# First chunk of a fused two-layer kernel: the order of its loads, its mean and variance by matmul alone, and later weight centring

## The chip, the cores and the metric

The kernel runs on one core of one Trainium2 chip. The metric is device time in microseconds (us) for one execution. The engines are named as the profile names them: PE is TensorE (matmuls), PEld its weight load, DVE is VectorE, ACT is ScalarE, POOL is GpSimd, and SP is the engine that issues most of the DMAs.

## The reference

The input x has 2 sequences of 1024 tokens with 256 channels. Eight blocks follow one another, four in each of two layers; pairs of them stand in a residual sum. In short:

```python
x = x + time_mix(adapter(x, profile_ids))         # layer 0: adapter chosen per sequence, linear recurrence
x = x + moe(mlp_with_chosen_part(x, ids))         # layer 0: 8 experts, 2 per token
x = x + local_attention(dense_or_sparse_attention(x))   # layer 1
x = x + squared_relu_ffn(adapter2(x, ids))        # layer 1
```

The change touches the first block. Its adapter is chosen by a profile number, one for each sequence (`itok_B_0_6`, two numbers below 8):

```python
z = relu(hidden @ Wd[id] + bd[id])                # 256 -> 128
y = hidden + z @ Wu[id] + bu[id]                  # 128 -> 256
mu = mean(y); var = mean((y - mu) ** 2)           # over the 256 channels
out = (y - mu) * rsqrt(var + 1e-5) * g[id] + b[id]
```

Its output goes into a token-shift mixer, four small projections, and the recurrence.

## The kernel before

x is kept transposed and resident: 128 partitions, two halves of the 256 channels, 2048 tokens (`x`, `[P, 2, T]`). The first block works on four chunks of 512 tokens (`CK`), two for each sequence. `tmix_in` runs three steps in a staggered way: while `adapt` works on chunk i, `mix` works on chunk i-1 and `project` on chunk i-2. Each step is a generator, and a string of letters says which one goes on next (`together`). A scheduler then sets the final order of each engine's queue from the written order and the dependences; each engine takes its own queue strictly from the front.

`setup` makes the constants and loads `vecs`, the packed vectors, on SP's queue. `program` then loads the four chunks of x on ACT's queue (L1796). `load_adapter0` reads the two profile numbers into a register of SP (`value_load`, L116; two dependent loads each) and with each number loads the packed weights of that sequence, `d0_0` and `d0_1` (L118). `load_attn0` loads `wa`, the weights of mixer and projections (L124), and `lvl`, a small table of masks (L126), which POOL then spreads 16 times (L129). `load_late` follows with `wf` and two more number reads (L156). Twelve zero fills of DRAM tables close this part of SP's queue (L1812).

`centre_weights` takes the mean out of the up-projection of each sequence, so that the adapter's output needs no second mean: DVE reduces `wu` and subtracts (L168 to L170), PE averages the bias `bu` with the matrix `avg`, which holds 1/256 everywhere (L173), and DVE subtracts that too (L174, L175). It does so for both sequences before the first chunk. `centre_values` does the same for the value weights in `wa` (L360 to L362), when `i == 1`.

`adapter_steps` is the adapter of one chunk. POOL adds the two channel halves of x (`both`, L202). PE makes `pz` (L205) and ACT the relu `z` (L207). PE makes the mean of x by one matmul of `avg` with `both` (L209), and DVE subtracts it from x (L212). PE makes the up-projection `py` (L217), DVE adds it and the bias (L219). ACT squares both halves in one instruction (L221), POOL adds the two squared halves (L223), PE makes the variance, four matmuls of 128 tokens each into columns of `nv` (L227). ACT takes the root and DVE the reciprocal (`inverse_root`, L181 and L183). PE transposes it to a row for each token (L234), DVE multiplies (L237) and ACT adds the offset into `q` (L238). The tiles named `ad` are two PSUM banks used in turn; `both` is one buffer. The profile counts two PE passes for each fp32 matmul.

Of the kernel before, what the change touches and what calls it, by code (L numbers as in the profile page):

```python
# [9 lines left out]
F32 = mybir.dt.float32  # L10
# [8 lines left out]
P = 128  # L19
B = 2  # L20
# [42 lines left out]
def tiles(tc, **how):  # L63

    return tc.tile_pool(reuse_waits="tile", **how)
# [24 lines left out]
def setup(k, ctx):  # L90
    nc, tc, ins = k.nc, k.tc, k.ins
    cp = ctx.enter_context(tiles(tc, name="const", bufs=1))
    k.vecs = cp.tile([P, NVEC], F32, name="vecs")
    nc.sync.dma_start(out=k.vecs, in_=ins["vecs"])
    k.ident = cp.tile([P, P], F32, name="ident")
    make_identity(nc, k.ident)
    k.avg = cp.tile([P, P], F32, name="avg")
    nc.vector.memset(k.avg, 1.0 / C)

    k.sel64 = cp.tile([P, 2], F32, name="sel64")  # L100
    nc.vector.memset(k.sel64, 0.0)
    for h in range(2):
        nc.vector.memset(k.sel64[64 * h : 64 * h + 64, h : h + 1], 1.0 / 64)
    k.ones = cp.tile([P, P], F32, name="ones")
    nc.vector.memset(k.ones, 1.0)
    k.eps = {}
    for n, e in (("ln", 1e-5), ("gn", 0.00064)):
        k.eps[n] = cp.tile([P, 1], F32, name=f"eps_{n}")
        nc.vector.memset(k.eps[n], e)


def load_adapter0(k, pool):
    nc, ins = k.nc, k.ins
    k.d0 = []
    for b in range(B):
        i = nc.sync.value_load(ins["ids"][0:1, b : b + 1], min_val=0, max_val=7)  # L116
        t = pool.tile([P, ND0], F32, name=f"d0_{b}")
        nc.sync.dma_start(out=t, in_=ins["d0"][bass.ds(i, 1)].rearrange("o p f -> p (o f)"))  # L118
        k.d0.append(t)


def load_attn0(k, pool, raw):
    k.wa = pool.tile([P, NWA], F32, name="wa")
    k.nc.sync.dma_start(out=k.wa, in_=k.ins["wa"])  # L124
    lvl = raw.tile([P, 6, P // 4], U8, name="lvl")
    k.nc.sync.dma_start(out=lvl, in_=k.ins["lvl"])  # L126

    k.lvl = pool.tile([P, 6, 2 * S // P, P // 4], U8, name="lvls")
    k.nc.gpsimd.tensor_copy(k.lvl, lvl.unsqueeze(2).to_broadcast([P, 6, 2 * S // P, P // 4]))  # L129


def load_cond2_0(k, pool):
# [26 lines left out]
        k.d2.append(t)  # L159


def centre_weights(k, sp, pp, packed, table, n_wu, n_bu):

    nc = k.nc
    for t in packed:
        wu, bu = (part(t, table, n) for n in (n_wu, n_bu))
        m = sp.tile([P, 2], F32, name="cwm")
        nc.vector.reduce_sum(m[:, 0:1], wu, axis=AX.X)  # L168
        nc.vector.tensor_scalar_mul(m[:, 0:1], m[:, 0:1], 1.0 / C)
        nc.vector.tensor_scalar(wu, wu, m[:, 0:1], None, ALU.subtract)  # L170
        pb = pp.tile([P, CK], F32, name="nv")
        for c in range(2):
            nc.tensor.matmul(pb[:, 0:1], lhsT=k.avg, rhs=bu[:, c : c + 1], start=c == 0, stop=c == 1)  # L173
        nc.vector.tensor_copy(m[:, 1:2], pb[:, 0:1])  # L174
        nc.vector.tensor_scalar(bu, bu, m[:, 1:2], None, ALU.subtract)  # L175
# [8 lines left out]
    return rs  # L184


def adapter_steps(k, sp, pp, x, ch, dst, tables, names, hid):

    nc = k.nc
    packed, table = tables
    n_wd, n_wu, n_bd, n_bu = names
    b, t0 = ch // 2, ch * CK
    ts = slice(t0, t0 + CK)
    nb = CK // P
    wd = part(packed[b], table, n_wd, 2)
    wu, bd, bu, g, bb = (part(packed[b], table, n) for n in (n_wu, n_bd, n_bu, "g", "b"))  # L200
    both = sp.tile([P, CK], F32, name="both")
    nc.gpsimd.tensor_add(both, x[:, 0, ts], x[:, 1, ts])  # L202
    pz = pp.tile([P, CK], F32, name="ad", bufs=2)
    for c in range(2):
        nc.tensor.matmul(pz, lhsT=wd[:, c, :], rhs=x[:, c, ts], start=c == 0, stop=c == 1)  # L205
    z = sp.tile([P, CK], F32, name="z")
    nc.scalar.activation(z, pz, AF.Relu, bias=bd)  # L207
    pm = pp.tile([P, CK], F32, name="ad", bufs=2)
    nc.tensor.matmul(pm, lhsT=k.avg, rhs=both, start=True, stop=True)  # L209
    y = sp.tile([P, 2, CK], F32, name="y")  # L210
    for c in range(2):
        nc.vector.tensor_sub(y[:, c, :], x[:, c, ts], pm)  # L212
    yield
    py = [pp.tile([P, CK], F32, name="ad", bufs=2) for c in range(2)]
    for c in range(2):
        hs = slice(0, hid) if hid == P else slice(c * hid, (c + 1) * hid)
        nc.tensor.matmul(py[c], lhsT=wu[hs, c * P : (c + 1) * P], rhs=z[hs], start=True, stop=True)  # L217
    for c in range(2):
        nc.vector.scalar_tensor_tensor(y[:, c, :], py[c], bu[:, c : c + 1], y[:, c, :], ALU.add, ALU.add)  # L219
    sq = sp.tile([P, 2, CK], F32, name="nsq")  # L220
    nc.scalar.activation(sq, y, AF.Square)  # L221
    both = sp.tile([P, CK], F32, name="both")
    nc.gpsimd.tensor_add(both, sq[:, 0, :], sq[:, 1, :])  # L223
    yield
    pv = pp.tile([P, nb], F32, name="nv")
    for j in range(nb):
        nc.tensor.matmul(  # L227
            pv[:, j : j + 1], lhsT=both[:, j * P : (j + 1) * P], rhs=k.avg[:, 0:1], start=True, stop=True
        )
    rs = inverse_root(k, sp, pv, "ln")  # L230
    yield
    pb = pp.tile([P, CK], F32, name="ad", bufs=2)
    for j in range(nb):
        nc.tensor.transpose(pb[:, j * P : (j + 1) * P], rs[:, j : j + 1].to_broadcast([P, P]), k.ident)  # L234
    for c in range(2):
        t = sp.tile([P, CK], F32, name="t")
        nc.vector.scalar_tensor_tensor(t, y[:, c, :], g[:, c : c + 1], pb, ALU.mult, ALU.mult)  # L237
        nc.scalar.activation(dst[:, c, :], t, AF.Identity, bias=bb[:, c : c + 1])  # L238
    yield


def adapted(k, sp, pp, x, it, tables, names, hid):

    q = it["q"] = sp.tile([P, 2, CK + 1], F32, name="q", bufs=2)
    if it["ch"] % 2:
        k.nc.vector.tensor_copy(q[:, :, 0:1], it["prev"]["q"][:, :, CK : CK + 1])
    else:
        k.nc.vector.memset(q[:, :, 0:1], 0.0)
    yield from adapter_steps(k, sp, pp, x, it["ch"], q[:, :, 1:], tables, names, hid)


def together(order, **steps):
# [6 lines left out]
def tmix_in(k, x, r, kk, w, v):  # L259
# [10 lines left out]
    with (  # L270
# [2 lines left out]
        tiles(tc, name="mxp", bufs=1, space=PSUM) as pp,  # L273
    ):

        centre_weights(k, sp, ap, k.d0, D0, "wu", "bu")

        def bank(i, shape=(P, CK)):
            return pp.tile(list(shape), F32, name=f"f{i}")

        def adapt(it):
            return adapted(k, sp, ap, x, it, (k.d0, D0), ("wd", "wu", "bd", "bu"), P)

        def mix(it):
            cur = it["q"][:, :, 1:]
# [69 lines left out]
        def centre_values():  # L355


            wv = part(wa, WA, "v").rearrange("p (g d) -> p g d", d=64)
            mean = sp.tile([P, 8], F32, name="wvm")
            nc.vector.reduce_sum(mean, wv, axis=AX.X)  # L360
            nc.vector.tensor_scalar_mul(mean, mean, 1.0 / 64)
            nc.vector.tensor_sub(wv, wv, mean.unsqueeze(2).to_broadcast([P, 8, 64]))  # L362

        its = [dict(ch=ch) for ch in range(NCK)]
        for i in range(NCK + 2):
            steps = {}
            if i == 1:
                centre_values()
            for n, at, step in (("a", i, adapt), ("m", i - 1, mix), ("p", i - 2, project)):
                if 0 <= at < NCK:  # L370
                    its[at]["prev"] = its[at - 1]
                    steps[n] = step(its[at])
            together("apmpapmppaamppp", **steps)
# [1408 lines left out]
def program(ctx: ExitStack, tc: tile.TileContext, ins, out):  # L1782
# [8 lines left out]
    x = xp.tile([P, 2, T], F32, name="x")  # L1791
    xv = ins["xT"].rearrange("(c p) t -> p c t", p=P)
    setup(k, ctx)
    for ch in range(NCK):
        ts = slice(ch * CK, (ch + 1) * CK)
        nc.scalar.dma_start(out=x[:, :, ts], in_=xv[:, :, ts])  # L1796

    lp = ctx.enter_context(tiles(tc, name="late", bufs=1))
    with tiles(tc, name="w0", bufs=1) as wp:
        load_adapter0(k, wp)  # L1800
        with tiles(tc, name="rkwv", bufs=1) as ap:
            r, kk, w = ([ap.tile([P, 2, S], F32, name=f"{n}{b}") for b in range(B)] for n in "rkw")
            v = ap.tile([P, NBLK, C], F32, name="v")
            with tiles(tc, name="zero", bufs=1) as zp:
                load_attn0(k, wp, zp)
                load_late(k, lp)
                z = zp.tile([P, ROW], F32, name="z")
                nc.vector.memset(z, 0.0)
                for t, n in ((xs, 2 * NSLOT), (ys, 2 * T)):
                    f = t.shape[-1]  # L1810
                    for i in range(n // 1024):
                        nc.sync.dma_start(  # L1812
                            out=t[i * 1024 : (i + 1) * 1024, :].rearrange("(p j) f -> p j f", p=P),
                            in_=z[:, 0:f].unsqueeze(1).to_broadcast([P, 8, f]),
                        )
                tmix_in(k, x, r, kk, w, v)
            with tiles(tc, name="y0", bufs=1) as yp:
                y = yp.tile([P, 2, T], F32, name="y")
                wkv(k, r, kk, w, v, y, x)
# [148 lines left out]
```

## Time and profile before

| what | value |
|---|---|
| three runs, us | 1516.82, 1510.14, 1517.79 |
| their median, us | 1516.82 |
| profiled execution's own time, us | 1515.27 |
| its span, us | 1513.6 |
| PE busy | 1414.6 us, 93% |
| DVE busy | 872.7 us, 58% |
| ACT busy | 680.9 us, 45% |
| POOL busy | 180.7 us, 12% |
| granted clock of PE, mean | 0.962 |
| DMA | 70.77 MB, mean 47 GB/s |

The span runs from the first to the last instruction of the program that the profiler saw; 1.67 us of the execution's own time lie around it. A timeline row gives start and length in us, engine, line of the kernel, operation, tile written and tiles read, shapes, how many instructions are merged, and in brackets how long the engine was idle before and what released it. A row of the waits gives who waited for whom: total us, times, longest. The granted clock is the share of PE's full clock that a throttle allowed; it is recorded from its first change on, so a stretch before that shows as 1.00.

### The profile page before, as it was taken

How to read it: one execution, taken by the hardware profiler on the slowest of the kernel's cores; microseconds unless marked ns; L12 is line 12 of the kernel's file. 1: busy time of each engine (PE TensorE's matmuls, PEld its weight loads, DVE VectorE, ACT ScalarE, POOL GpSimd, SP SyncE). 2: the span in 40 equal slices, each digit the busy share in tenths (PEclk: the TensorE clock that was granted, in tenths of full speed). 3: DMA queues.
4: the chain of work that ended last, by engine and by line, in shares of the span. 5: the costliest groups of instructions: out<-in, count | busy, mean ns of one | idle time of the engine just before them, and what ended most of it. 6: DMA issues, size and time to landing. Idle time of an engine off the chain costs nothing. (4 is left out here: it accounts for less than half of the span.)

```text
span 1513.6 us, 27333 instructions
## 1 busy us (share of the span) xinstructions
PE 1414.6 (93%) x10778; PEld 964.2 (64%) x10778; DVE 872.7 (58%) x2774; ACT 680.9 (45%) x1681; POOL 180.7 (12%) x167
## 2 busy tenths in 40 slices
PE   5998889999699999968999999999999999999998
PEld 2445877445456766635666645788886457878866
DVE  3545834121489931157887713787884247778764
ACT  2443143222122122117888721766674337656733
POOL 1523630022411121110000000000000000000011
PEclk9899589999899999979999999999999999999999
DMA  9500004300353332030000010000000000000001
GB/s 307 188 1 2 5 2 154 125 30 30 95 166 120 127 129 82 18 121 1 2 2 2 29 56 1 2 2 2 1 2 1 0 0 2 2 1 2 2 15 44
DMA packets 42758, 70.77 MB, mean 47 GB/s; under 512 B 7168, under 2 KB 35840, under 8 KB 39552
## 3 DMA queue, kind: packets, MB, share of 16 engines
q1 hardware_dynamic: 35776, 55.55, 11.0%
q0 software_dynamic: 3072, 8.65, 1.6%
q10 hardware_dynamic: 3776, 4.75, 1.0%
q8 instruction: 87, 1.43, 0.4%
q14 instruction: 47, 0.39, 0.1%
HBM read 45.09 MB, written 23.86 MB: 46 GB/s over the span
## 5 line engine op out<-in xcount | busy, mean ns | idle before, releaser
L1617 ACT ACTIVATE pe<-pe,nm 128x320 f32<-128x320 f32 x256 | 141.8, 555 | 131.1 <-DVE nm L1607 130.9
L1607 DVE CUSTOM_DVE_ANT_0 pe<-ps,wbs 128x320 f32<-128x320 f32 x256 | 118.5, 486 | 6.1 <-PE ps L1601 1.8
L1229 ACT ACTIVATE pe<-pe,nm 128x256 f32<-128x256 f32 x256 | 110.4, 498 | 20.4 <-DVE nm L1219 20.4
L965 PE MATMUL ph<-xt,w 128*128 128x512 f32 x256 | 113.8, 602 | 2.7 <-ACT xt L960 2.7
L1597 PE MATMUL ps<-kT,qT 64*128 64x384 f32 (+1 forms) x512 | 110.2, 498 | 3.3 <-DVE qT L1571 2.9
L973 PE MATMUL po<-w,h 128*128 128x256 f32 x512 | 111.8, 379 | 0.0
L973 PEld LDWEIGHTS po<-w,h 128*128 128x128 f32 x512 | 97.3, 190 | 16.6 <-issue 3.3
L1219 DVE CUSTOM_DVE_ANT_0 pe<-ps,lc 128x256 f32<-128x256 f32 x256 | 94.2, 417 | 21.0 <-PE ps L1203 19.3
L1666 PE MATMUL py<-ptt,v 128*64 128x128 f32 x1408 | 103.6, 277 | 0.1
L895 DVE SCALAR_TENSOR_TENSOR lc<-iok,idx,lc 128x256 f32<-128x256 f32 x248 | 102.2, 475 | 0.3
L965 PEld LDWEIGHTS ph<-xt,w 128*128 128x128 f32 x256 | 48.6, 193 | 62.6 <-issue 55.7
L1666 PEld LDWEIGHTS py<-ptt,v 128*64 128x64 f32 x1408 | 78.6, 137 | 11.3 <-issue 8.3
L1639 PE MATMUL pt<-ident,pe 128*128 128x128 f32 x512 | 79.8, 282 | 1.9 <-DVE pe L1625 0.9
L1238 PE MATMUL ptp<-ident,pe 128*128 128x128 f32 x512 | 73.8, 283 | 5.7 <-ACT pe L1229 2.9
L1238 PEld LDWEIGHTS ptp<-ident,pe 128*128 128x128 f32 x512 | 55.8, 142 | 33.1 <-ACT pe L1229 16.8
L968 ACT ACTIVATE h<-ph,vecs 128x512 f32<-128x512 f32 x64 | 44.0, 687 | 71.3 <-PE ph L965 70.2
L1626 ACT ACTIVATE pe<-pe,rd 128x320 f32<-128x320 f32 x128 | 70.8, 558 | 8.9 <-DVE rd L1624 8.9
L1601 PEld LDWEIGHTS ps<-sk,qT 64*128 64x128 f32 x512 | 50.9, 187 | 26.2 <-issue 0.3
L1646 DVE TENSOR_TENSOR ptt<-pt,tri 128x512 f32<-128x512 f32 x96 | 64.8, 675 | 0.0
L1639 PEld LDWEIGHTS pt<-ident,pe 128*128 128x128 f32 x512 | 56.1, 140 | 10.9 <-issue 2.0
L976 DVE TENSOR_TENSOR ye<-po,b 128x256 f32<-128x256 f32 x32 | 13.4, 419 | 82.4 <-PE po L973 82.4
L1688 PE MATMUL ps<-yT,w1ao 128*128 128x256 f32 x256 | 59.0, 385 | 0.7
(355 smaller groups left out, 2743.5 us busy)
## 6 DMA issues: line engine op xcount, KB each, us to landing
w<-in_mw SPq DMA_DIRECT2D x16, 1024.0 KB, 5.2
xs<-z SPq DMA_DIRECT2D x8, 1088.0 KB, 11.8
ys<-z SPq DMA_DIRECT2D x4, 1024.0 KB, 11.6
xe<-xs SPq DMA_DIRECT2D x7, 544.0 KB, 6.3
more<-xs SPq DMA_DIRECT2D x7, 544.0 KB, 4.0
x<-in_xT ACTq DMA_DIRECT2D x4, 512.0 KB, 5.9
g<-ys ACTq DMA_DIRECT2D x4, 512.0 KB, 6.0
out_x<-o SPq DMA_DIRECT2D x8, 256.0 KB, 2.2
```

The lines of the kernel that those rows point to most:

```text
L895: nc.vector.scalar_tensor_tensor(n, key, k.idx[:, qb, j : j + 1], n, ALU.is_equal, ALU.add)
L965: nc.tensor.matmul(ph, lhsT=w1[:, c, m * P : (m + 1) * P], rhs=xt[:, c, :], start=c == 0, stop=c == 1)
L973: nc.tensor.matmul(po, lhsT=h[:, m, j * P : (j + 1) * P], rhs=w2[:, m, :], start=m == 0, stop=m == 7)
L1219: nc.vector.tensor_tensor_reduce(out=pe[:, j, :], in0=it["ps"][i][:, j, :], in1=k.lc[:, q0 + j, :], scale=-1.0, scalar=3.0e38, op0=ALU.add ...
L1229: nc.scalar.activation(pe[:, j, :], pe[:, j, :], AF.Exp, bias=nm, scale=-1.0)
L1238: nc.tensor.transpose(ptp[:, kb, j, :], it["pe"][i][:, j, kb * P : (kb + 1) * P], k.ident)
L1597: nc.tensor.matmul(ps[:, i, keys[i]], lhsT=qs[i], rhs=kT[hp, m + pair, k0 : k0 + nk], start=True, stop=True)
L1607: nc.vector.tensor_tensor_reduce(out=pe[:, i], in0=ps[:, i, used[i]], in1=wbs[:, 0 if n == 0 else 3 if n == NB - 1 else 1 + i, (1 - i) * G ...
L1617: nc.scalar.activation(pe[:, i], pe[:, i], AF.Exp, bias=nm[:, i : i + 1], scale=-1.0, accum_out=den[:, i : i + 1])
L1626: nc.scalar.activation(pe[:, 1], pe[:, 1], AF.Copy, scale=rd[:, 1:2])
L1639: nc.tensor.transpose(pt[1 - j if i and inner(n) else j][:, 2 * pair + i, :], pe[:, at : at + P], k.ident)
L1666: nc.tensor.matmul(py[64 * i : 64 * i + 64, (m + pair) % 4, :], lhsT=keys[:, hs], rhs=it["pts"][:, pair, :] if j == 3 else it["pt"][:, j, ...
```

## The change

Loads: ACT's queue carries the first chunk of x alone. On SP's queue the profile number of sequence 0 is read first and `d0_0` loaded, then come chunk 1 of x, `vecs` and `wa`, then the number and weights of sequence 1, then chunks 2 and 3, then `lvl` and the rest as before. The spread of `lvl` on POOL is written after `tmix_in`; in the built order it stands in POOL's queue behind the sum of chunk 1's halves and ahead of the sum of chunk 1's squares.

Chunk 0 alone gets another form of the adapter (`direct`): the mean is two accumulating matmuls on the halves of x, ahead of `pz`; the centring of sequence 0's weights is written between `z` and `py`; the square is done half by half; the variance is eight matmuls, two accumulating for each 128 tokens, with no sum on POOL.

Centring for sequence 1 and of the value weights is written at `i == 2` and no longer before chunk 0 and at `i == 1`; their means use buffers of `m` and `xm` instead of own ones. In the built order, value centring runs on DVE between chunk 1's additions (L219) and the first products of `mix` (L308), and centring for sequence 1 stands on PE just ahead of chunk 2's `pz`. On ACT, `z` of chunk 2 now stands ahead of the second `q` of chunk 1. Of the parts of the program behind `wkv`, nothing is changed in the source.

```diff
-def load_adapter0(k, pool):
...
+def load_adapter0(k, pool, b):
+    i = nc.sync.value_load(ins["ids"][0:1, b : b + 1], min_val=0, max_val=7)
+    t = pool.tile([P, ND0], F32, name=f"d0_{b}")
+    nc.sync.dma_start(out=t, in_=ins["d0"][bass.ds(i, 1)].rearrange("o p f -> p (o f)"))
+    return t
...
-def centre_weights(k, sp, pp, packed, table, n_wu, n_bu):
+def centre_weights(k, sp, pp, packed, table, n_wu, n_bu, mean=None, bank=dict(name="nv")):
...
-        m = sp.tile([P, 2], F32, name="cwm")
+        m = mean or sp.tile([P, 2], F32, name="cwm")
...
-        pb = pp.tile([P, CK], F32, name="nv")
+        pb = pp.tile([P, CK], F32, **bank)
...
-    both = sp.tile([P, CK], F32, name="both")
-    nc.gpsimd.tensor_add(both, x[:, 0, ts], x[:, 1, ts])
+    y = sp.tile([P, 2, CK], F32, name="y")
+
+    def halves(t):
+        if direct:
+            return [t[:, c, :] for c in range(2)]
+        both = sp.tile([P, CK], F32, name="both")
+        nc.gpsimd.tensor_add(both, t[:, 0, :], t[:, 1, :])
+        return [both]
+
+    def centred(parts):
+        pm = pp.tile([P, CK], F32, name="ad", bufs=2)
+        for i, t in enumerate(parts):
+            nc.tensor.matmul(pm, lhsT=k.avg, rhs=t, start=i == 0, stop=i == len(parts) - 1)
+        for c in range(2):
+            nc.vector.tensor_sub(y[:, c, :], x[:, c, ts], pm)
+
+    parts = halves(x[:, :, ts])
+    if direct:
+        centred(parts)
...
-    pm = pp.tile([P, CK], F32, name="ad", bufs=2)
-    nc.tensor.matmul(pm, lhsT=k.avg, rhs=both, start=True, stop=True)
-    y = sp.tile([P, 2, CK], F32, name="y")
-    for c in range(2):
-        nc.vector.tensor_sub(y[:, c, :], x[:, c, ts], pm)
+    if direct:
+        direct()
+    else:
+        centred(parts)
...
-    nc.scalar.activation(sq, y, AF.Square)
-    both = sp.tile([P, CK], F32, name="both")
-    nc.gpsimd.tensor_add(both, sq[:, 0, :], sq[:, 1, :])
+    for cs in (slice(0, 1), slice(1, 2)) if direct else (slice(0, 2),):
+        nc.scalar.activation(sq[:, cs, :], y[:, cs, :], AF.Square)
+    parts = halves(sq)
...
-        nc.tensor.matmul(
-            pv[:, j : j + 1], lhsT=both[:, j * P : (j + 1) * P], rhs=k.avg[:, 0:1], start=True, stop=True
-        )
+        for i, t in enumerate(parts):
+            nc.tensor.matmul(
+                pv[:, j : j + 1],
+                lhsT=t[:, j * P : (j + 1) * P],
+                rhs=k.avg[:, 0:1],
+                start=i == 0,
+                stop=i == len(parts) - 1,
+            )
...
-        centre_weights(k, sp, ap, k.d0, D0, "wu", "bu")
+        def centre(b, mean=None, **bank):
+            centre_weights(k, sp, ap, k.d0[b : b + 1], D0, "wu", "bu", mean, bank)
...
+            direct = (lambda: centre(0, name="ad", bufs=2)) if it["ch"] == 0 else None
...
-            mean = sp.tile([P, 8], F32, name="wvm")
+            mean = sp.tile([P, 2, CK], F32, name="xm")[:, 0, 0:8]
...
-            if i == 1:
+            if i == 2:
+                centre(1, sp.tile([P, CK], F32, name="m"), name="nv")
                 centre_values()
...
-    for ch in range(NCK):
+
+    def load_x(queue, ch):
         ts = slice(ch * CK, (ch + 1) * CK)
-        nc.scalar.dma_start(out=x[:, :, ts], in_=xv[:, :, ts])
-
+        queue.dma_start(out=x[:, :, ts], in_=xv[:, :, ts])
+
+    load_x(nc.scalar, 0)
...
-        load_adapter0(k, wp)
+        k.d0 = [load_adapter0(k, wp, 0)]
+        load_x(nc.sync, 1)
+        nc.sync.dma_start(out=k.vecs, in_=ins["vecs"])
+        load_attn0(k, wp)
+        k.d0.append(load_adapter0(k, wp, 1))
+        for ch in range(2, NCK):
+            load_x(nc.sync, ch)
...
-                load_attn0(k, wp, zp)
+                spread_levels = load_levels(k, wp, zp)
...
                 tmix_in(k, x, r, kk, w, v)
+                spread_levels()
```

## The prediction on record before the run

> **What bounds the kernel now.** I read the page first, then the waits of the first 30 us, the timeline of the first 41 us, the reads of the profile numbers, and the busy time by stretches.
>
> ```profile
> span 1513.6 us, 27333 instructions
> ...
> PE   5998889999699999968999999999999999999998
> ```
>
> TensorE (PE) is the bound: busy 93% of the span, and only the first slice (37.8 us) falls to five tenths. The change touches little beyond that slice, so the question is who ends last there.
>
> ```profile
> PE nv L173 <- DMA d<-in_d: 10.6, 1, 10.6
> PEld nv L227 <- POOL both L223: 4.8, 1, 4.8
> POOL both L223 <- ACT nsq L221: 4.7, 1, 4.7
> ```
>
> PE does nothing for 10.6 us, until the packed weights of sequence 0 (`d0_0`) land; later it waits for GpSimd (POOL), which adds the two squared halves.
>
> ```profile
> 5.08 1.26 POOL L202 TENSOR_TENSOR both<-x 128x512 f32<-128x512 f32 x1 [3.69 <-DMA x<-in_xT]
> 10.60 0.98 PE L173 MATMUL nv<-d,avg 128*128 128x1 f32 x4 [10.60 <-DMA d<-in_d]
> 14.01 2.06 PE L205 MATMUL ad<-x,d 128*128 128x512 f32 x2
> 16.10 0.69 ACT L207 ACTIVATE z<-ad,d 128x512 f32<-128x512 f32 x1 [4.28 <-PE ad L205]
> 21.70 1.06 ACT L221 ACTIVATE nsq<-y 128x1024 f32<-128x1024 f32 x1 [4.91 <-DVE y L219]
> 24.15 1.87 PE L227 MATMUL nv<-avg,both 128*128 128x1 f32 x8 [4.02 <-POOL both L223]
> 26.58 1.12 PE L234 MATMUL ad<-ident,nrs 128*128 128x128 f32 x4 [0.57 <-DVE nrs L183]
> 27.49 3.62 PE L205 MATMUL ad<-x,d 128*128 128x512 f32 x4
> ```
>
> This is one chain for chunk 0: weights, centring, `pz`, `z`, `y`, squares, variance, inverse root. The first chunk of x was there by 5.08. The last row but one, 26.58, is my marker T: from there chunk 1 follows as before.
>
> ```profile
> 17.30:24.20 6.90, 2.36 (x6) 1.00 0.79 248
> 24.20:31.00 6.80, 6.23 (x17) 0.50 1.12 351
> ```
>
> Here the columns are PE busy, granted clock, DMA share and GB/s. At a clock of 0.50 a 128x512 pass follows the last by 0.855 us (four in 3.62, at 27.49). At full clock the step is 0.43 (eight L326 passes in 3.60 at 126.89). A 128x1 pass takes 0.217 at half clock (eight in 1.87) and about 0.125 at full clock (eight in 1.05, at 1172.06). Before 17.3 the rows took the half-clock steps, so PE came to full clock 6.7 us after its first matmul, and lost it again at 24.2.
>
> ```profile
> 60.00:130.00 70.00, 68.16 (x214) 33.33 (x213) 32.10 (x48) 27.96 (x42) 32.76 (x29) 0.95 0.00 0
> ```
>
> From 60 to 130 PE (first figure) is busy 97% and no DMA runs, so what the first 60 us save or lose passes to the end.
>
> **The change, part by part.**
>
> *Landings.* The read of profile number 0 stands behind `vecs` on SP and takes two loads:
>
> ```profile
> L116 SPq TENSOR_LOAD <-in_ids_ptr x2: 1026/1499/1972, 1.3 to 5.5; - x2
> L116 SPq TENSOR_LOAD <-in_ids x2: 476/1342/2209, 2.3 to 7.5; - x2
> ```
>
> With `vecs` gone it starts at 0.82 and not 1.28, with one chunk of x in flight instead of four. The first load stays 1.03; the second lies between 0.48 and 2.21, and I take its median of 1.34. With 0.5 for register work, `d0_0` is issued at 3.7 (2.8 to 4.6), not 5.04. The four `d` loads landed 2.6 to 5.4 after issue, three of them by 2.8; with less traffic I take 2.8. So `d0_0` lands at about 6.5 (5.4 to 10.0), not 10.5. Chunk 0 of x landed 4.2 after its issue with three chunks behind it; a half as large `d` needs 2.6. I take 3.6, nearer the row of its own size: 4.4 (3.4 to 5.0).
>
> *Mean ahead of weights.* The mean is now two matmuls on x itself, so PE starts at 4.45. Four half-clock passes end at 7.9, which hides `d0_0` up to there. Then `pz`: four passes, to 11.3. If full clock again comes 6.7 us after the first matmul, that is at 11.2, so `z` starts at 11.5 and ends at 12.2 (before: 16.8). The reduce and two scalings of `d0_0` (0.42+0.15+0.35, VectorE, DVE) lie under the mean; the bias centring (four 128x1 passes) lies under `z`, and would cost 0.5 if `z` were earlier.
>
> *From z to the squares.* `py` is four full-clock passes, 12.4 to 14.3. The second no longer waits for the subtraction (row L217 had 0.5 of that), and the 1.5 us of value centring (L360 to L362) no longer stand between the two adds. The adds (0.74 each) end at 15.15. The square is split; its second half (about 0.55) ends at 15.75, while the first is done beside the second add.
>
> *Variance without GpSimd.* The 1.26 us POOL sum goes; eight passes become sixteen, of which 14 follow the second square. At full clock: 14 x 0.125 plus a tail of 0.15 ends at 17.7. At half clock it would be 3.4, to 19.2, as much as POOL and eight passes took together (22.8 to 26.0). I take full clock, since PE had dense work within 2 us. The table load (1.28) fits beside it. Root, reciprocal and the rest took 0.57 in the old rows, so T = 18.3. **Gain: 26.6 - 18.3 = 8.3 us.**
>
> *What is moved behind.* Value centring now reuses `xm`, so it waits for `pa` (L295, ends 37.9); behind it on DVE stand the `xw` products, idle until 39.77. 0.68+0.17+0.68 = 1.5 fits in those 1.9: I take nothing (0 to 1.5 if the cover is gone). Centring for sequence 1 puts four 128x1 passes on PE before `pz` of chunk 2, in a stretch where PE was busy 9.4 of 10.3 us: 0.5 to 0.9, I take **0.7 us**. A gain is excluded, since PE has no idle time there to take them. Its DVE work (0 to 1.3) goes into gaps of 0.6 to 1.7 around `xx`: nothing. The built order also puts `z` of chunk 2 before chunk 1's second `q` on ScalarE (ACT); PE does `py` first and `pa` after it, which covers this (see rivals).
>
> *The SP queue.* Second chunk, `vecs` and `wa` go behind `d0_0`, then the second number's read (2.5 to 5.3 by the L116 and L156 rows), `d0_1`, two chunks, `lvl`, `wf`, two more reads and the zero fills. All x bytes now share SP's queue, yet each user is late: chunk 1 at T, `wa` and `vecs` near 27, chunk 2 near 36, `d0_1` near 40, against landings of some 7, 11, 15 and 14. The fills start up to 2 us later; their last landed at 59.2, and nothing reads there before 215. `eye` now waits for POOL's spread of `lvl`, which is done about 100 us earlier. All nothing.
>
> **Sum.** 8.3 - 0.7 = 7.6 us less. Against the profiled execution's own 1515.27 this gives **1507.7**. That execution is 1.55 below the median of 1516.82; from the median the same sum gives 1509.2. The runs before spread over 7.7 us. A measurement of this kernel can tell about 0.5%, 7.6 us, so the sum stands right on that bound.
>
> The first matmul at 10.60 and full clock at 17.3 are 6.7 us apart. [...]
>
> **Rivals.**
>
> - *Half clock throughout.* The old rows held half clock for 6.7 us and lost it after thin work. If PE stays there until T: `z` ends at 12.2, `py` at 16.0, adds 16.8, square 17.4, variance 20.8, T = 21.4. Gain 5.2 - 0.7 = 4.5: 1510.8. [...] Against: the new start is seven dense microseconds. Chance 0.15.
> - *Full clock early.* If PE is released when the mean ends (7.9), `pz` is over by 9.8, `z` by 10.5, `py` by 12.6, the second square by 14.0; of the variance some nine passes fall back to half clock, and T = 17.4: 9.2 - 0.7 = 8.5, 1506.8. Chance 0.12. [...]
> - *The number is not read sooner.* If the load stays 2.21 and the landing 5.4, `d0_0` lands at 10.0, as good as before. Then `pz` starts at 10.05; with full clock at 11.2 it ends at 12.5, T = 19.3: 7.3 - 0.7 = 6.6, 1508.7. Chance 0.08.
> - *Given back in chunk 2.* The second `q` of chunk 1 waits for `z` of chunk 2, up to 3.3 us later than now (it was at 50.0, `z` ended at 52.7). If `xm` is late at PE, that much is lost: 1511.0. Against: PE has six passes of L326 and L217 in between. Chance 0.10.
> - *Slower: POOL stands behind `lvl`.* The spread (L129, 2.74) is ahead of chunk 1's sum of squares on POOL, and `lvl` is now issued after a second read and two chunks. It decides when `lvl` lands after about 29; each us beyond delays PE's L227 by one, the gain is gone at a landing near 38 and the kernel over 0.5% slower (1524.4) from 46 on. Landing at 50 would give 1529. Before, it landed at 15.3, 6.0 after issue; by the rows I expect 18. Chance 0.05.
>
> **Numbers.** The forecast has 0.50. Against 1509.2 and the scatter of runs I count as faster 0.31 of it, 0.09 of early clock, 0.05 of the late number, 0.04 of half clock and 0.02 of chunk 2: 0.51. Slower is POOL's 0.05; the remaining 0.44 is within 0.5%. The range takes in 1506.8 to 1511.0 and some 3 us of scatter on each side (half the spread of the runs before, less what the cases overlap): 1503 to 1514.
>
> **What would show it.** Right: PE's first row at about 4.5 from x, not `d`; L173 for `d0_0` hidden; `z` near 11.5; no POOL row before the variance passes; L234 near 18.3; stretches after 60 equal but shifted. Wrong: PE waiting for `d` after its first four passes, `pz` steps that are not 0.855, the sixteen variance passes over 2.5 us, `pa` idle before chunk 2's `py`, POOL waiting for `lvl` beyond 29, or a gain at T that is gone by 60.

## The result, and the profile after

| | changed kernel | kernel before |
|---|---|---|
| median, us | 1512.5 (20 runs, 1507.26 to 1518.53) | 1516.71 (20 runs, 1510.14 to 1524.36) |
| profiled execution, its own time and span, us | 1508.30, 1506.6 | 1515.27, 1513.6 |
| T, first transpose of chunk 0's root, us | 17.85 | 26.58 |

The ratio is 0.9971 (95% interval 0.9957 to 0.9985): faster, by 4.2 us between the medians, where 7.6 were forecast. The time lies in the range on record. The two profiled executions differ by 6.97 us, nearly the forecast sum, but they are one draw each from runs that spread over 11 and 14 us. Counting twelve more runs of the changed kernel, from the first experiment, the mean of 32 is 1512.4 ± 0.6 (± is the standard error); the 67 runs of the kernel before that stand beside them have 1516.6 ± 0.4, which makes the gain 4.2 ± 0.8. In the four programs that are cut short further below, 12 of 22 runs count as slow, that is, over 1.5% above the fastest run of their kernel, and the means there take in all of them; the fast runs alone differ by 6.4 us at the first cut and 1.5 at the second. So there are two questions: is the gain at T real, and where do some 4 us of it go?

The changed kernel's page, span and PE's slices:

```profile
span 1506.6 us, 27352 instructions
...
PE   6998989999599999959999999999999999999998
```

The first slice rises from five tenths to six; nothing else stands out. The waits of the first 30 us:

```profile
PE ad L212 <- DMA x<-in_xT: 4.9, 1, 4.9
...
PEld nv L243 <- ACT nsq L237: 2.0, 2, 1.5
```

PE starts at 4.9 from x and not at 10.6 from `d`. The two waits of 4.7 and 4.8 us through POOL have become 2.0 from ACT. The timeline of chunk 0's chain (start, length, engine, line):

```profile
4.87 3.75 PE L212 MATMUL ad<-x,avg 128*128 128x512 f32 x4 [4.87 <-DMA x<-in_xT]
...
8.42 2.67 PE L221 MATMUL ad<-x,d 128*128 128x512 f32 x4
...
11.12 0.69 ACT L223 ACTIVATE z<-ad,d 128x512 f32<-128x512 f32 x1 [3.06 <-PE ad L221]
...
14.67 0.63 ACT L237 ACTIVATE nsq<-y 128x512 f32<-128x512 f32 x1 [0.23 <-DVE y L234]
...
15.35 1.83 PE L243 MATMUL nv<-avg,nsq 128*128 128x1 f32 x14 [0.47 <-ACT nsq L237]
...
17.85 1.08 PE L254 MATMUL ad<-ident,nrs 128*128 128x128 f32 x4 [0.66 <-DVE nrs L182]
17.88 2.74 POOL L128 COPY lvls<-lvl 128x3072 uint8<-128x3072 uint8 x1 [7.83 <-DMA lvl<-in_lvl]
...
18.73 3.62 PE L221 MATMUL ad<-x,d 128*128 128x512 f32 x4
```

The mean hides the landing of `d0_0` (DVE's first row from it is at 6.73); the sixteen variance passes (two more at 14.50) run at full clock, 0.13 each; POOL's spread of `lvl` starts at 17.88, far from the 29 at which it would begin to count. The busy time by stretches (length, then PE, PEld, DVE, ACT and POOL busy, granted clock, DMA share, GB/s):

```profile
10.00:17.00 7.00, 5.44 (x27) 3.42 (x25) 1.89 (x4) 3.23 (x4) 0.06 (x1) 0.99 0.95 342
17.00:20.40 3.40, 2.74 (x7) 1.69 (x8) 0.93 (x2) 0.91 (x2) 2.52 (x1) 0.50 0.65 252
...
60.00:130.00 70.00, 68.18 (x210) 33.71 (x205) 30.84 (x46) 29.47 (x46) 26.91 (x24) 0.95 0.00 1
```

The clock is full from 10.0 to 16.8 and halved behind (0.50, to 23.65), and the stretch from 60 to 130 is as dense as before (68.18 us of PE, 68.16 before). Row by row the changed trace runs 8.8 us ahead through chunk 1, 8.26 ahead at the recurrence's first matmul (132.94 against 141.20), 7.35 ahead at its last output, and 7 at the end. In this pair 7.0 of the 8.73 us reach the end.

### The profile page after: what moved, and what is told of

Its sections match the earlier page's. It is cut to its first block, busy times and chain, and to the rows that moved or that the text cites. A ratio compares the mean times of both kernels' runs of the same rounds, so it can differ in the third digit from the quotient of the medians.

```text
span 1506.6 us, 27352 instructions
## 1 busy us (share of the span) xinstructions
PE 1417.6 (94%) x10788; PEld 966.4 (64%) x10788; DVE 874.6 (58%) x2774; ACT 681.1 (45%) x1682; POOL 178.7 (12%) x165
## 3 DMA queue, kind: packets, MB, share of 16 engines
q1 hardware_dynamic: 36592, 57.12, 11.3%
## 5 line engine op out<-in xcount | busy, mean ns | idle before, releaser
L1252 ACT ACTIVATE pe<-pe,nm 128x256 f32<-128x256 f32 x256 | 110.4, 498 | 20.5 <-DVE nm L1242 20.5
L996 PEld LDWEIGHTS po<-w,h 128*128 128x128 f32 x512 | 97.3, 190 | 16.6 <-issue 3.3
L1689 PEld LDWEIGHTS py<-ptt,v 128*64 128x64 f32 x1408 | 78.7, 137 | 11.3 <-issue 8.4
L1662 PEld LDWEIGHTS pt<-ident,pe 128*128 128x128 f32 x512 | 56.1, 140 | 11.2 <-issue 2.0
```

Of the source, the lines that this page charges most:

```text
L996: nc.tensor.matmul(po, lhsT=h[:, m, j * P : (j + 1) * P], rhs=w2[:, m, :], start=m == 0, stop=m == 7)
L1252: nc.scalar.activation(pe[:, j, :], pe[:, j, :], AF.Exp, bias=nm, scale=-1.0)
L1662: nc.tensor.transpose(pt[1 - j if i and inner(n) else j][:, 2 * pair + i, :], pe[:, at : at + P], k.ident)
L1689: nc.tensor.matmul(py[64 * i : 64 * i + 64, (m + pair) % 4, :], lhsT=keys[:, hs], rhs=it["pts"][:, pair, :] if j == 3 else it["pt"][:, j, ...
```

## The experiments

The theories named in the expectations: **A**, the gain is whole and only hidden by the scatter of the clock; **B**, the clock's windows (in both traces the granted clock changes at whole multiples of 3.41 us from its first change on) often fall so in the first chunk that T gains less; **C**, it is given back later. Then, once C stood, for the recurrence: **P**, it depends on the moment at which the recurrence begins; **L**, chance of the clock; **F**, the place of a stall of PE; **M**, extra matmuls cost by themselves. F was named ahead of the six runs that test it. The kernel before itself had means from 1515.0 to 1517.9 us on the chips used here, so a time is set against runs of the kernel before on the same chip.

### Both kernels again

Nothing altered.

> The changed kernel unaltered, for a second trace of it and for more times beside the kernel before. Theory A (scatter of the clock): T, the start of the transposes of chunk 0 (L254), is again within 1.5 us of 17.85, the shift against the kernel before at 130 us is about 8, and the time differs from 1508.3 because the granted clock behind 130 us differs, by about 1 us for each 0.001 of mean clock. Theory B (phase of the clock windows in the first chunk): T itself moves by 2 us or more, to 19 to 21.4. Theory C (given back): T near 17.85, but the shift at 60 us is below 6.

> The kernel before unaltered, for a second trace of it. A: T (start of the transposes, L234) within 1 us of 26.58, and the time moves with the clock behind 130 us. B: T falls to 24.5 to 25.5, since the clock is released earlier than 17.3 when its windows fall otherwise; then the profiled pair overstated the gain by 1 to 2 us. Ratio to the kernel before 1.000 plus or minus 0.0015 under all theories.

Measured: 1513.21 us (12 runs; ratio 0.9982, 0.9964 to 1.0) and 1516.15 us (12 runs; ratio 1.0005, 0.9985 to 1.0026). T was 17.9 and 26.3. The gain at T is there again, and the total gain is small again. Two copies of one kernel differ by 0.05%; the interval reaches from -0.15% to 0.26%.

### The loads alone, the new form of chunk 0 alone

`loads_only`, against the changed kernel (new load order and late centring, old form of chunk 0):

```diff
+        centre(0, name="nv")
...
-            direct = (lambda: centre(0, name="ad", bufs=2)) if it["ch"] == 0 else None
+            direct = None
```

`direct_only` keeps the new form and puts `vecs` and all four chunks of x back ahead of the number's read, and the second sequence's weights ahead of `wa`, as in the kernel before:

```diff
-    load_x(nc.scalar, 0)
+    nc.sync.dma_start(out=k.vecs, in_=ins["vecs"])
+    for ch in range(NCK):
+        load_x(nc.scalar, ch)
...
```

> The changed order of the loads and the late centring, with the old form of the first chunk: mean and variance with POOL's sums, sequence 0 centred ahead of the chunk. The weights land at 6.7 instead of 10.5, the centring of sequence 1 (0.85 of PE) and the value centring (0.8) are out of the chain. T should be 26.6 - 3.8 - 1.6 = 21.2, and the shift at 130 us about 5. If the loads do nothing for the time, T stays above 25. Time 1511.5 by A, 1513 by B.

> The changed form of the first chunk and the late centring, with the loads in the old order (vectors first, all chunks of x on ACT, numbers after). Weights land at 10.5 again. PE does the mean from 5.0 to 8.5 and then waits; pz from 10.5. T = 10.5 + 2.6 to 3.4 for pz + about 6.6 from there (11.1 to 17.85 in the changed kernel) = 20 to 21; shift at 130 us 5.5 to 6.5. If the form does nothing beside the loads, T is above 24.5. Time 1511 by A, 1512.5 by B.

Measured: T = 20.8 in both; 1512.36 us (ratio 0.9977, 0.9955 to 1.0) and 1510.21 us (0.9968, 0.9945 to 0.9992), means 1512.3 ± 1.2 and 1511.6 ± 1.3. Each part alone brings T 5.8 us forward, and the two together 8.7: part of each hides under the other. In time they can't be told from one another or from the whole change.

### The program cut off behind the mixing, and behind the recurrence

`to_mix` ends when `r`, `k`, `w` and `v` are written and leaves out the recurrence and all behind it; `to_wkv` ends with the recurrence and leaves out the rest. Each was made from both kernels; shown is `to_mix`, while `to_wkv` writes 2 MB of `x` instead:

```diff
-                wkv(k, r, kk, w, v, y, x)
...
+            nc.sync.dma_start(out=out.rearrange("(n p) c -> p n c", p=P), in_=v)
```

> The kernel before, ended after the mixing and projections (about 135 us): recurrence and all later blocks are left out, and the value tiles are copied to the output. For its time alone, against after_to_mix: many runs without the later scatter. About 150 us. Theory A (the gain is 8 us in every execution): after_to_mix is 7.5 to 9.5 us shorter in the mean. Theory B (the phase of the clock windows in the first 130 us; the traces overstated it): 4 to 5.5 us shorter, as in the whole kernel. Theory C (given back behind): 7.5 to 9.5 here as in A, but less at the end of the recurrence.

> The changed kernel with the same end: recurrence and later blocks left out. T (L254) at 17.5 to 18.3 by all theories. Time below before_to_mix by 7.5 to 9.5 us (A and C) or by 4 to 5.5 us (B).

> The kernel before, ended after the recurrence and its output product (about 270 us): all later blocks left out, the first 2 MB of state copied to the output. About 290 us, with a scatter of several us from the clock. A: after_to_wkv is 7 to 9 us shorter in the mean. B: 4 to 5.5. C (the recurrence gives it back): 4 to 5 here although 7.5 to 9.5 at the end of the mixing.

> The changed kernel with the same end after the recurrence: later blocks left out. Below before_to_wkv by 7 to 9 us (A), 4 to 5.5 (B and C; C only if the two kernels that end after the mixing differ by 7.5 or more).

Measured, means of 6, 6, 6 and 4 runs: 151.56 ± 0.75 against 143.81 ± 0.69 to the end of the mixing, and 284.01 ± 1.46 against 279.41 ± 0.84 to the end of the recurrence. So 7.75 ± 1.0 us of gain leave the first stage, which is against B, and the whole program has 4.2 ± 0.8, which is against A: C holds. At the end of the recurrence 4.6 ± 1.7 are left. That points at the recurrence, none of whose lines is touched by the change, but the loss of 3.1 ± 2.0 between the two cuts is weak by itself; the traces below have to bear it out.

### The recurrence begun later

`after_wait1` and `after_wait2` repeat the first scaling of `ru` on ACT once and twice, `before_wait2` does it twice in the kernel before:

```diff
-                    nc.scalar.activation(ru[:, c, :], r[b][:, c, :], AF.Copy, scale=k.vec("u", c))
+                    for _ in range(1 + (1 if b == c == 0 else 0)):
+                        nc.scalar.activation(ru[:, c, :], r[b][:, c, :], AF.Copy, scale=k.vec("u", c))
```

> The changed kernel with the first scaling of r by u (ACT, 1.07 us) done twice ahead of the recurrence, so that PE enters it 1.07 us later; the values are the same. In the traces so far, the stretch from the last value tile to the last addition of the recurrence took 105 us plus 0.53 of the time at half clock, which was 51.2 to 54.6 us in the kernel before (132 us) and 51.2, 61.4 and 68.3 in the changed one (133 to 140). Theory P (where PE enters the recurrence against the clock windows decides how often it drops to half clock): the mean moves by something other than 1.07, by 2 us or more either way, and the half-clock time with it. Theory L (a lottery that has nothing to do with the entry): mean of the changed kernel, 1512.4, plus 1.07 = 1513.5, within 1.5.

> The same with the scaling done three times, so entry 2.13 us later. P: the mean is off 1512.4 + 2.1 by 2 us or more, perhaps below the changed kernel itself. L: 1514.5 within 1.5.

> The kernel before with entry into the recurrence 2.13 us later, in the same way. P: the half-clock time in the recurrence rises above 51.2 to 54.6 and the mean is 1520 or more, as the changed kernel's, shifted. L: 1516.5 + 2.1 = 1518.6 within 1.5.

Measured: 1511.65 us (0.9975, 0.9963 to 0.9987), 1514.89 us (1.0001, 0.9989 to 1.0013) and 1520.58 us (1.0042, 1.0022 to 1.0062). The wait came out twice as long as I had planned: the recurrence began 2.1 and 4.2 us later. By the means, with the 33 runs of the kernel before on the same chip (1515.1 ± 0.4) as the measure, the changed kernel is 3.6 ± 0.8 us below it with the first delay and 0.1 ± 0.7 with the second, against 4.2 ± 0.8 without: the delays cost 0.6 ± 1.1 and 4.1 ± 1.1 us. In the kernel before 4.2 us cost 5.5 ± 1.4. None of the three costs is clearly off the plain delay, and none of these moments brings the lost gain back, so P gets no support. It is not ruled out: `before_wait2` had a mean above 1520 and 63.7 us at half clock in its recurrence, the signs that P had named; yet that recurrence took 130.6 us, as short as any.

### The clock started early

`warm_start` puts eight constant matmuls ahead of chunk 0, while PE waits for x:

```diff
+        warm = pp.tile([P, CK], F32, name="f0")
+        for _ in range(8):
+            nc.tensor.matmul(warm[:, 0:P], lhsT=k.avg, rhs=k.ones, start=True, stop=True)
```

> The changed kernel with eight 128x128 matmuls of constants on PE from about 1.3 us on, until the first chunk of x lands; their results are not used. For the half-clock term: the clock was released 5.1 to 6 us after PE's first matmul. If that holds it comes near 7 instead of 10: the mean ends at 8.1, pz at 10 and T is 16.2 to 16.8 instead of 17.85; z at 9.7 to 10.3. If the constant 128x128 work does not count, T stays at 17.8. For the whole time: L says 1512.4 - 1.3 = 1511.1; P says anything from 1508 to 1515, since the entry into the recurrence moves too.

Measured: 1510.24 us (ratio 0.9963, 0.9949 to 0.9977), T = 15.8; full clock from 5.4 us, 4.1 after PE's first matmul at 1.3. It brings T 2.0 forward. The changed kernel was not run beside it; against the kernel before, `warm_start` is 5.7 ± 0.8 us below and the changed kernel 4.2 ± 0.8. The stall described next stands at pass 367 in it, still ahead of a level's end.

### The stall that moves

The traces then showed one thing that differs within the recurrence. It begins with 256 passes of PE for the diagonals; then come six levels, each of 128 passes for either sequence. PE stops for nothing that the trace names ("issue") at places 127 or 128 passes apart. Not every such place shows a stop: of fifteen, eight do in the kernel before (at passes 138, 266, 394, 521 and four later ones) and four in the changed one (383, 511, 893 and 1785). These are timeline rows of PE, first of the kernel before, then of the changed kernel, around the first levels, and under each the first product of POOL and of DVE that waits for a level's last pass (`decay` multiplies `k` on POOL and `r` on DVE):

```profile
147.23 0.32 PE L432 MATMUL sc<-r,k 64*64 64x32 f32 x8 [0.30 <-DVE A L420]
147.91 2.07 PE L432 MATMUL sc<-r,k 64*64 64x32 f32 x128 [0.36 <-issue]
151.37 1.95 PE L432 MATMUL sc<-r,k 64*64 64x32 f32 x118 [1.39 <-issue]
154.11 0.50 PE L432 MATMUL sc<-r,k 64*64 64x32 f32 x9 [0.80 <-DVE r L461]
...
150.05 2.83 POOL L460 TENSOR_TENSOR k<-k,w 128x1024 f32<-128x1024 f32 x1 [21.08 <-PE sc L432]
...
152.20 1.77 DVE L461 TENSOR_TENSOR r<-r,w 128x1024 f32<-128x1024 f32 x1
```

```profile
138.98 2.06 PE L455 MATMUL sc<-r,k 64*64 64x32 f32 x125 [0.30 <-DVE A L443]
141.97 2.06 PE L455 MATMUL sc<-r,k 64*64 64x32 f32 x128 [0.93 <-issue]
145.42 0.24 PE L455 MATMUL sc<-r,k 64*64 64x32 f32 x1 [1.39 <-issue]
146.77 5.49 PE L455 MATMUL sc<-r,k 64*64 64x32 f32 x184 [1.11 <-DVE r L484]
...
142.73 2.82 POOL L483 TENSOR_TENSOR k<-k,w 128x1024 f32<-128x1024 f32 x1 [22.01 <-PE sc L455]
...
143.37 3.26 DVE L484 TENSOR_TENSOR r<-r,w 128x1024 f32<-128x1024 f32 x1
```

Before, the stall falls some ten passes into the next level (8 passes, stall, 128 passes, stall); the level that just ended is complete, and the others work on. After, it falls ahead of the very last pass (128 passes, stall, 1 pass): a level that is otherwise done waits 0.93 or 1.39 us for it. Then PE waits for DVE's `r` in both, 0.80 before and 1.11 after. Counted from the recurrence's first pass, the stall stands at pass 394 before and 383 after: the change puts ten more passes ahead, and in `loads_only`, which adds none, it stands at 393. POOL starts 9.79 us behind that first pass instead of 8.85 (142.73 - 132.94, 150.05 - 141.20), and DVE's product, which does not end until 1.08 us after POOL's, takes 3.26 instead of 1.77. Theory F is that this is the loss. By F, a few tiny matmuls at PE's start, where PE is idle, must move the stall, and the time with it.

`before_shift`, `before_few` and `before_ten` are the kernel before with six, two and ten of them (two passes each); `after_sum` takes eight passes out of the changed kernel by adding chunk 0's two squares on DVE (one more instruction, 0.69 us); `after_sum_shift` puts four tiny matmuls back; `sum_warm` has two of 512 columns instead:

```diff
+        warm = pp.tile([P, CK], F32, name="f0")
+        for _ in range(6):
+            nc.tensor.matmul(warm[:, 0:1], lhsT=k.avg, rhs=k.ones[:, 0:1], start=True, stop=True)
```

```diff
-    parts = halves(sq)
+    if direct:
+        both = sp.tile([P, CK], F32, name="both")
+        nc.vector.tensor_add(both, sq[:, 0, :], sq[:, 1, :])
+        parts = [both]
+    else:
+        parts = halves(sq)
```

> The kernel before with six fp32 matmuls of one column (12 passes) put at PE's start, where it waits for the first load: T stays at 26 us. Theory F (place of PE's stall): the stall moves from pass 394 of the recurrence to about pass 382, GpSimd's first product starts near 9.6 us behind the first pass instead of 8.85, the stage of the levels takes 59.5 to 61 us instead of 57 to 58.5, and the time rises to 1518 to 1520. Theory L (chance of the clock): the stall moves, but the levels stay at 57 to 59 and the time at 1515 to 1517.

> The changed kernel with the two squares of chunk 0 added on VectorE (0.63 us or so) and half of the variance's passes (8 fewer): T within 0.4 us of 17.85. Theory F: the stall moves from pass 383 to about pass 391, behind the end of the level; the levels take 57 to 58.5 us instead of 59.4 to 61.4, and the time falls to 1508 to 1510.5. Theory L: the levels stay as in the changed kernel and the time at 1511.5 to 1513.5.

> after_sum with four fp32 matmuls of one column (8 passes) at PE's start, nothing else: T as in after_sum. Theory F: the stall is back at pass 383, the levels take 59.4 to 61.4 us, and the time is 2 to 4 us above after_sum, 1511 to 1514. Theory L: no difference from after_sum beyond 1 us.

> after_sum with two fp32 matmuls of 512 columns (4 passes, about 3.7 us at half clock) from 1 us on, which start the clock early as the eight of warm_start did: T 15.5 to 16.2. Theory F: the stall sits at about pass 387, still behind the end of the level, the levels take 57 to 58.5 us and the time is 1505.5 to 1508. Theory L: as warm_start, 1509 to 1510.

> The kernel before with two fp32 matmuls of one column (4 passes) at PE's start. Theory F (place of PE's stall): the stall moves from pass 394 to about 390, still behind the end of a level; from the recurrence's first pass to its last output 130.5 to 133.5 us, and the time within 1 us of the kernel before. Theory M (such matmuls cost by themselves): 1 us or more above it.

> The kernel before with ten such matmuls (20 passes). Theory F: the stall sits at about pass 374, ten passes ahead of the end of a level; the recurrence takes 133 to 137 us and the time is 2 to 4 us above the kernel before. Theory L (chance of the clock): 130.5 to 133.5 us as likely as not, and the time within 1 us of the kernel before.

Measured (the first four against 27 runs of the kernel before, median 1517.36 and mean 1517.9 ± 0.7; the last two against 23, 1516.21 and 1517.0 ± 0.6):

| kernel | stall at pass | median, us | mean, us | ratio to before (interval) | T |
|---|---|---|---|---|---|
| before_shift | 382 | 1520.43 | 1520.0 ± 0.9 | 1.001 (0.9989 to 1.0031) | 26.4 |
| after_sum | 391 | 1508.69 | 1509.0 ± 0.9 | 0.9935 (0.9914 to 0.9956) | 16.6 |
| after_sum_shift | 383 | 1512.73 | 1511.9 ± 0.9 | 0.9959 (0.9939 to 0.9979) | 17.8 |
| sum_warm | 387 | 1505.87 | 1506.6 ± 0.8 | 0.992 (0.9894 to 0.9946) | 15.9 |
| before_few | 390 | 1516.37 | 1515.8 ± 1.0 | 0.9992 (0.9975 to 1.001) | 26.7 |
| before_ten | 374 | 1520.92 | 1519.4 ± 1.1 | 1.0018 (0.9997 to 1.0038) | 26.0 |

Passes 384, 512 and so on begin a level. The stall went where the count said, pass for pass: 12, 4 and 20 passes ahead, eight back, eight ahead again. Six matmuls cost 2.1 ± 1.1 us and ten 2.4 ± 1.3; two, which leave the stall behind the end of a level, cost nothing (-1.2 ± 1.2), which speaks against M; four added to `after_sum` cost 2.8 ± 1.3.

Each by itself is weak, and the intervals of the first and the last ratio reach below 1; the three contrasts together give 2.4 ± 0.7 us for a stall ahead of a level's end. There is a fourth that does not fit: `direct_only` (stall at 383) against `loads_only` (393), at the same T, gives -0.7 ± 1.8; all four together give 2.0 ± 0.7. A small cost of each extra matmul beside that (M) is not excluded by these errors. Single profiles did not all come as F expected: the levels took 59.7 us in `after_sum`, where stalls of 0.9 us at passes 135 and 263 made PE late, and 58.5 in `after_sum_shift`, less than in `after_sum` and not the 59.4 to 61.4 expected; the recurrence took 131.6 in `before_ten`; and POOL's first product in `before_shift` started 8.88 us behind the first pass, not near 9.6.

Part of `after_sum`'s lead is the clock, which in its profile was full from 7.7 us on and put T at 16.6, 1.2 ahead of `after_sum_shift`; how much of the 2.8 us that makes in the mean of the runs is not known.

PE's rows of `after_sum`, then of `after_sum_shift`, at the same level:

```profile
139.34 2.48 PE L460 MATMUL sc<-r,k 64*64 64x32 f32 x128 [0.88 <-issue]
143.34 6.87 PE L460 MATMUL sc<-r,k 64*64 64x32 f32 x248 [1.52 <-issue]
```

```profile
145.43 0.19 PE L464 MATMUL sc<-r,k 64*64 64x32 f32 x1 [1.39 <-issue]
146.37 5.84 PE L464 MATMUL sc<-r,k 64*64 64x32 f32 x254 [0.76 <-DVE r L493]
```

With the stall ahead of the last pass, a wait for DVE's `r` of 0.76 follows it; with the stall behind, PE runs on through this level. That is not so in every execution: `before_few`, with the stall behind, has a wait of 1.31 for `r` there.

The length of the recurrence itself, from its first pass to the start of the addition that makes the last output tile, in every profile of this case that has it:

| stall | executions, us |
|---|---|
| behind a level's end | before 131.0, again 130.8, to_wkv 131.5, wait2 130.6; loads_only 130.4; after_sum 133.5; sum_warm 130.8; before_few 130.6 |
| ahead of it | after 131.9, again 137.2, to_wkv 138.5, wait1 136.4, wait2 136.5; direct_only 133.9; warm_start 134.1; before_shift 134.3; after_sum_shift 134.9; before_ten 131.6 |

The means are 131.2 and 134.9, 3.8 ± 0.9 apart. Twelve of the 18 are the executions that F was drawn from; the six made afterwards to test it (after_sum, sum_warm and before_few against before_shift, after_sum_shift and before_ten) differ by 2.0 ± 1.4. Part of the 3.8 is the levels themselves: fitted over the 18 executions, they take 1.7 ± 0.4 us longer for the same time at half clock. The rest lies behind the levels. There the stretch to the last output is told by the clock alone: 67.4 us plus 0.32 for each us at half clock fits all 18 within 0.4 us. These are the two parts, levels and what follows, of the kernel before and of the second profile of the changed one:

```profile
141.18:198.28 57.10, 47.22 (x1920) 45.15 (x1920) 43.87 (x50) 15.81 (x31) 34.23 (x14) 0.73 0.02 5
198.28:272.18 73.90, 68.24 (x749) 51.78 (x750) 27.55 (x50) 24.48 (x46) 7.23 (x15) 0.86 0.32 106
```

```profile
130.95:190.95 60.00, 48.11 (x1920) 45.74 (x1920) 44.41 (x49) 15.63 (x31) 34.64 (x14) 0.75 0.02 4
190.95:268.15 77.20, 71.46 (x749) 54.23 (x750) 28.03 (x50) 24.63 (x47) 7.80 (x15) 0.80 0.31 100
```

In this pair the levels lose 2.9 us at a slightly higher clock (0.75 against 0.73); the second part loses 3.3 us at a lower one (0.80 against 0.86). With the stall ahead, six of ten executions had 24 to 31 us of half clock in the second part; with the stall behind, none of eight had over 20.5. That the thinner work of the levels brings the clock down behind them is argued from these counts, not shown by a run. L, chance alone, would have to give all four contrasts together, 3 standard errors; it is unlikely as the whole, but chance remains: the changed kernel's first profile had 13.7 us of half clock there, which is why it showed 7 us of gain.

## Why the prediction was right or wrong

**The chain of the first chunk: right.** A gain of 8.3 us was worked out and 8.73 came. Step by step, forecast and measured: x at 4.45 and 4.87; `d0_0` issued 3.7 and 3.92, landed 6.5 and 6.71; `pz` ended 11.3 and 11.1; `z` 11.5 and 11.12; second square ended 15.75 and 15.3; variance ended 17.7 and 17.18; T 18.3 and 17.85. Each step from `pz` on lies 0.2 to 0.5 early, although x came 0.4 late: the clock came 5.1 us after the first matmul instead of 6.7. That it comes out so near is in part luck, since in other programs that begin alike full clock came from 2.8 (`after_to_wkv`) to 6.1 us (`after_wait2`) after it.

**What was moved behind: right.** Value centring stands on DVE from 29.20 to 30.81, and the first `xw` waits 0.19 for it. Centring for sequence 1 takes 1.01 on PE at 38.44; the lead of 8.76 moves between 7.4 and 10.0, with half clock from 33.9 to 44.1 in the changed kernel and from 41.2 to 51.5 in the one before, and is 8.26 at the recurrence, 0.5 less where 0.7 was taken. ACT's later `q` is covered, as was said.

**The failed step** is "what the first 60 us save or lose passes to the end". I had read it from how dense PE is from 60 to 130, and that part held: 7.75 ± 1.0 us came out of the mixing, 7.6 forecast. But behind lies the recurrence, whose PE waits and is awaited, and which has no term in the sum. It was taken as nothing, without a reason of its own; in its place the runs show a loss of 3.6 ± 1.3 us behind the mixing (7.75 ± 1.0 of gain at its end, 4.2 ± 0.8 at the program's). The stall's new place, at 2.0 to 2.4 ± 0.7, is the likely cause of the larger part; the rest is within the errors and stays open. Of the 4.8 us between the 1507.7 forecast and the 1512.5 measured, 1.55 come from something else: the sum was taken off one execution that lay that much below the median. With the stall in like places the forecast gain is there: `after_sum` is 8.9 ± 1.2 below the kernel before, `after_sum_shift` 8.2 ± 1.3 below `before_shift`. `direct_only` (stall ahead) does not fit well, as said: by F it should lie 2.0 to 2.4 above `loads_only`, and it lay 0.7 ± 1.8 below.

**The rivals.** Half clock throughout falls (14 variance passes in 1.83 us, not 3.4); so does the late number (`d0_0` at 6.71), and POOL behind `lvl` (17.88). Full clock early was half true: it came at 10.0, where this rival had 7.9 and the sum 11.2. "Given back in chunk 2" has a time, 1511.0, that lies nearer the measured one than the sum does, but by luck: by chunk 2 no more than the 0.5 above is given back, and the loss comes behind the mixing. The sign to look for, "stretches after 60 equal but shifted", was met by the stretch from 60 to 130 in the profiled pair: only many runs, and programs cut short, showed the loss.

## What to carry to other kernels

An edit that adds or removes a few instructions on PE also moved, for the recurrence behind it, where PE's stalls fall. The levels here take 128 passes and the stalls lie 127 or 128 apart, and in the changed kernel the bad place was hit again: 383, 511, 893 and 1785 lie 1, 1, 3 and 7 passes ahead of a level's end. In such a loop a handful of idle instructions at the start, or a few fewer, may be worth as much as a real saving: `sum_warm`, which starts the clock early and keeps the stall behind the end, took 1505.87 us in six runs, 0.8% less than the kernel before on the same chip. When a stage's saving should pass on unchanged, cut the program at the stage's end and at the next one's and time both; one profiled pair cannot show a loss of 3 us where runs of one kernel spread over 11.

## What the runs showed of the hardware

PE's stall: at places 127 or 128 pairs of weight load and matmul apart, though not at each of them, and 0.27 to 2.0 us long in the recurrence of the two kernels. Its place follows the count of passes ahead (4, 8, 12 and 20 tried). What PE waits for there, no run shows.

DVE's product and POOL's: in the first four pairs of products that wait for PE's passes, in both kernels, DVE's `r` product ended 1.07 to 1.10 us after POOL's `k` product. So the first took what was left of POOL's plus 1.08 us, 0.68 + 1.08 in the kernel before (row: 1.77), 2.18 + 1.08 after (3.26). In the three pairs behind them DVE's ended 1.77 to 1.83 us ahead of POOL's and took 1.21 to 1.87. What ties the two, no run shows.

The clock: full 2.9 us after PE's first matmul in `after_sum`, 4.1 in `warm_start`, 5.1 in the changed kernel, 6.7 in the one before; the recorded stretches at half clock are multiples of 3.41 us, from 3.41 to 34.13 in the two kernels, but for those that the end of the program cuts.
